# The last stage of a twelve-layer kernel: branch first, eight places, two queues, one root for all tiles

## The chip, the cores and the metric

The kernel runs on one core of one Trainium2 chip. The core has five engines with a queue of instructions each: TensorE (PE, with its weight loads PEld), VectorE (DVE), ScalarE (ACT), GpSimd (POOL) and SyncE (SP), which here only issues transfers. Transfers are issued from the queues of SP, ACT and POOL and carried out by the core's 16 DMA engines. The metric is the time of one execution in microseconds of the device; the median of several executions counts. Profiles come from one more execution each.

## The reference, cut to what matters

The program is a stack of four levels, each with a cross attention, an attention and a feed-forward layer with experts, on 1024 rows (32 x 32) of 256 columns. The change is in the last layer alone:

```python
def _rmsnorm(x, w):
    var = jnp.mean(x * x, axis=-1, keepdims=True)
    return w * (x * jax.lax.rsqrt(var + EPS_NORM))
...
src = x + _gqa(x, qw, qb, kw, kb, vw, vb, ow, ob)
src = _rmsnorm(src, norm1_w)
src = src + _moe(src, gate_w, w1, w2)
return _rmsnorm(src, norm2_w)
...
x = x + _L3_ffn_ref(...)
return x
```

`_moe` sends every row to two of eight experts and adds their two results, weighted, to the row.

## The kernel before, in words

The 1024 rows lie in eight tiles of 128 rows by 256 columns: `self.x` holds the running result, `r.h` (called `src` in the last layer; the program's name for its storage is `rows`) the layer's own copy, four tiles in each of two buffers. NT is 8, HT is 4, NH is 2, K is 2.

The last layer, `l3_ffn`, does its attention and norm, and scatters the rows into places by expert. `experts` (from line 1973) runs over eight slots: it loads weights and rows on SP's queue, multiplies on PE, and writes each result row to the table `yk` in HBM, by indirect transfers from POOL's queue (line 2009). What follows is the stretch that the change rewrites:

- `outputs` (lines 2126 to 2134), still within the pool of the experts: for each of the eight tiles, SP loads the two result rows of each row from `yk` (256 KB, tile `gy`, four places in turn, line 2132), and VectorE adds them with their weights to `r.h`, one instruction for each k (line 2134).
- `rest` (lines 2136 to 2154): the general case in which an expert got more rows than its slot holds. A flag is computed early; every engine loads it (line 2151), compares and jumps (line 2152). With these inputs the body is jumped over. An engine that jumps then writes its semaphore up by what the body would have added; others wait for these values.
- `rms_half` (lines 2350 to 2359), once for each half of four tiles: four squares with sums on ACT (line 2356), the root by `rsqrt` on VectorE (lines 152 to 157, eleven small instructions on 128x4), four products with root and row on VectorE, in place (line 2359).
- four additions to `x` on POOL for each half (line 2409).
- in `tile_perceiver`, eight stores from SP (line 2428).

The instructions are recorded through a framework that places semaphores and tracks which buffers are in use; where no order is fixed by hand (`tc.manual_schedule`), it may put independent instructions of one engine in another order, as it does with the two halves' roots. When a pool is closed and another one opened on the same memory, the first writer of the new one waits for all users of the old one. Line 2491 is the end of the program: SP waits for the semaphores of all transfers, every engine drains, and they meet at a barrier.

Of the kernel before, what the change touches and what calls it, by code (L numbers as in the profile page):

```python
# [17 lines left out]
AF = mybir.ActivationFunctionType  # L18
ALU = mybir.AluOpType
# [3 lines left out]
P = 128  # L23
B, S, D = 32, 32, 256
NT = B * S // P
NH = 2
HT = NT // NH
# [40 lines left out]
class Kernel:  # L68
# [78 lines left out]
    def rsqrt(self, var, n, eps, scale=1.0):  # L147


        nc = self.nc  # L150
        a, r, u = (self.t(self.small, [P, HT], x)[:, 0:n] for x in ("rs_a", "rs_r", "rs_u"))
        nc.vector.tensor_scalar(a, var, scale, eps, ALU.mult, ALU.add)  # L152
        nc.vector.tensor_scalar(r.bitcast(I32), a.bitcast(I32), -0.5, float(0x5F3759DF), ALU.mult, ALU.add)  # L153
        for _ in range(3):
            nc.vector.tensor_mul(u, r, r)  # L155
            nc.vector.scalar_tensor_tensor(u, u, -0.5, a, ALU.mult, ALU.mult)  # L156
            nc.vector.scalar_tensor_tensor(r, u, 1.5, r, ALU.add, ALU.mult)  # L157
        return r
# [2199 lines left out]
        for i, s in enumerate(tiles):  # L2358
            nc.vector.scalar_tensor_tensor(s, s, r[:, i : i + 1], row, ALU.mult, ALU.mult)  # L2359

    def l3_ffn(self):
        nc, a, tc = self.nc, self.a, self.tc
        pre = "L3_ffn_"
        vb, ob, n1, n2 = (self.load_row(pre + n) for n in ("vb", "ob", "norm1_w", "norm2_w"))
        gw = self.load_w(a[pre + "gate_w"], "gw", 1)
        net = lambda r: (512, a[pre + "w1"], a[pre + "w2"], None, AF.Gelu, r.h, None)
        with tc.tile_pool(name="f3r", bufs=1) as outer:
            r = self.routing(outer, 8, 2, ((3, 112),) * 4 + ((2, 112), (2, 80), (1, 128), (1, 64)), CAPACITY)
            src = r.h
            hT = self.norm_T(self.x, src)  # L2370
            hT2 = []
            for i in range(NT):
                nc.gpsimd.tensor_tensor(src[i], src[i], ob, ALU.add)

            def end(i, ps):
                nc.vector.tensor_tensor(src[i], ps, src[i], ALU.add)

            def done(t0, n):

                part = slice(t0, t0 + n)  # L2380
                self.rms_half(src[part], n1)
                if t0 % HT == 0:
                    hT2.append(self.t(self.act, [P, 2, 512], "hT", 3))
                for i, s in enumerate(src[part]):
                    self.transpose_tile(s, hT2[-1], (t0 + i) % HT * P)
                W = [P, n, 8]
                pr, comb = r.lg[:, part, :], r.comb[:, part, :]
                self.gates(pr, hT2[-1], gw, 8, None, t0 % HT)
                nc.scalar.activation(pr, pr, AF.Sigmoid)
                m, _ = self.top(outer, pr, 8, 2, r.before[:, part, :])  # L2390
                nc.vector.tensor_tensor(comb, pr, m, ALU.mult)
                s = self.t(self.small, [P, HT], "wo_r", 1)[:, 0:n]
                nc.vector.reduce_sum(s, comb, axis=AX.X)
                nc.vector.tensor_scalar(s, s, 1e-6, None, ALU.add)
                nc.vector.reciprocal(s, s)
                nc.vector.tensor_tensor(comb, comb, s.unsqueeze(2).to_broadcast(W), ALU.mult)
                self.route(r, t0, n, m)

            self.qk_attn(pre, ("qw", "kw", "vw", "ow"), hT, pre + "qb", pre + "kb", vb, self.soft_max(0.25), False, end, done)
            with tc.tile_pool(name="f3m", bufs=1) as pool:  # L2400
                self.big = pool
                self.experts(pool, r, *net(r))
                self.outputs(pool, r, r.h, range(NT))
            self.rest(r, hT2, *net(r))
            for hf in range(NH):
                half = src[hf * HT : (hf + 1) * HT]
                self.rms_half(half, n2)
                for s, x in zip(half, self.x[hf * HT : (hf + 1) * HT]):
                    nc.gpsimd.tensor_tensor(x, x, s, ALU.add)  # L2409


@with_exitstack
def tile_perceiver(ctx: ExitStack, tc: tile.TileContext, a: dict, out: bass.AP):
    k = Kernel(ctx, tc, a)
    k.setup()
    k.load_ctx()
    k.xattn_heads(0)
    k.same_rows()
    k.clear_places()
    k.l0_attn()  # L2420
    k.l0_ffn()
    k.l1()
    k.l2()
    k.xattn_one()
    k.l3_attn()
    k.l3_ffn()
    for i in range(NT):
        tc.nc.sync.dma_start(out[i * P : (i + 1) * P, :], k.x[i])


# [64 lines left out]
```

## Time and profile before

| what | value |
|---|---|
| median of three runs | 1991.59 us (1985.03 to 1997.29) |
| the profiled execution's own time | 1987.18 us |
| its span | 1985.4 us |
| instructions | 40586 |
| busy share of the span: PE, DVE, ACT, POOL | 78%, 52%, 29%, 22% |
| granted TensorE clock, mean | 0.872 |
| last scatter to `yk` issued (line 2009) | 1951.25 us from the span's start |
| first load of `gy` issued (line 2132) | 1954.94 |
| last store issued (line 2428) | 1980.0 |

A time within the span is counted from the span's start. A line of the timeline gives start, length, engine, line of the code, operation, what is written and read, how many instructions were merged, and in brackets the idle time before it with what ended it. SPq, ACTq and the like are an engine's queue: transfers, branches and semaphores rather than computation. The page's shares are averages over all layers; this change has to be read from the last 35 us.

### The profile page before, as it was taken

What the parts mean: (1) busy time and instruction counts of PE and PEld (TensorE: products, weight loads), DVE (VectorE), ACT (ScalarE), POOL (GpSimd) and SP (SyncE); (2) the same over time, 40 slices, a digit from 0 to 9 for tenths busy, and PEclk for the clock granted to TensorE, in tenths of its full rate; (3) what the DMA queues carried; (4) which work ended last, traced back from release to release, by engine and by line L of the source; (5) the groups of instructions that cost most, each with busy time, mean ns of one, the idle gap of its engine ahead of it and who ended that gap; (6) DMA issues with size and microseconds to landing.
All of it is one profiled execution on the core that took longest, in us unless ns stands there. A gap on an engine that the chain in (4) does not pass through costs nothing. (4 is left out here: it accounts for less than half of the span.)

```text
span 1985.4 us, 40586 instructions
## 1 busy us (share of the span) xinstructions
PE 1543.9 (78%) x16098; PEld 1073.2 (54%) x16098; DVE 1031.1 (52%) x3295; ACT 582.4 (29%) x1631; POOL 433.0 (22%) x467
## 2 busy tenths in 40 slices
PE   6888879767999698766399689996894758777492
PEld 3555556544678365545277456655563634445372
DVE  6787764554111577656722264548624345555514
ACT  2443435521322366522122133430010212212121
POOL 2222211213011244330412211111312320120322
PEclk9999989876999899887699879998996979876596
DMA  9600001204443321011447621101102632000233
GB/s 279 189 2 1 7 22 44 71 8 146 139 145 112 129 66 55 26 64 60 149 155 212 184 83 41 33 25 52 27 13 74 207 119 86 2 2 2 92 124 116
DMA packets 117879, 167.01 MB, mean 84 GB/s; under 512 B 20272, under 2 KB 79676, under 8 KB 117664
## 3 DMA queue, kind: packets, MB, share of 16 engines
q1 hardware_dynamic: 106352, 140.59, 23.0%
q0 software_dynamic: 8144, 17.75, 2.5%
q10 hardware_dynamic: 3168, 5.79, 0.8%
q8 instruction: 137, 2.24, 0.5%
q14 instruction: 78, 0.64, 0.1%
HBM read 118.55 MB, written 48.84 MB: 84 GB/s over the span
## 5 line engine op out<-in xcount | busy, mean ns | idle before, releaser
L106 PE MATMUL mm<-e,hid 128*128 128x256 f32 (+4 forms) x984 | 231.2, 384 | 0.2
L106 PEld LDWEIGHTS mm<-e,hid 128*128 128x128 f32 (+4 forms) x984 | 172.4, 179 | 39.1 <-issue 1.3
L106 PE MATMUL sc<-xT,e 128*128 128x256 f32 (+8 forms) x736 | 179.8, 394 | 17.4 <-issue 12.8
L2009 POOL DMA_INDIRECT yk<-ys,to x98 | 92.8, 947 | 360.4 <-DVE ys L2007 189.4
L106 PEld LDWEIGHTS sc<-xT,e 128*128 128x128 f32 x736 | 130.0, 194 | 61.0 <-issue 24.7
L576 POOL TENSOR_TENSOR p<-p,over 128x512 f32<-128x512 f32 x80 | 102.8, 1293 | 254.6 <-DVE over L574 237.0
L563 ACT ACTIVATE p<-sc,less 128x256 f32<-128x256 f32 x256 | 117.9, 476 | 80.5 <-DVE less L555 49.0
L1879 POOL DMA_INDIRECT xg<-rows,pl_at x72 | 71.3, 990 | 223.7 <-DVE pl_at L1875 134.5
L106 PE MATMUL mm<-hT,w 128*128 128x512 f32 (+1 forms) x272 | 110.6, 566 | 7.7 <-ACT hT L356 7.7
L2110 ACT ACTIVATE hid<-sc,b1s 128x256 f32<-128x256 f32 (+6 forms) x152 | 72.2, 475 | 127.6 <-PE sc L106 126.6
L106 PE MATMUL mm<-ctxA,w 128*128 128x256 f32 x256 | 78.9, 427 | 18.8 <-DVE aT L607 7.4
L2007 DVE TENSOR_TENSOR ys<-mm,b2r 128x512 f32<-128x512 f32 (+6 forms) x44 | 28.2, 641 | 124.7 <-PE mm L106 124.3
L552 DVE TENSOR_REDUCE most<-sc 128x4 f32<-128x1024 f32 x64 | 77.9, 1217 | 18.6 <-PE sc L106 18.6
L106 PEld LDWEIGHTS mm<-hT,w 128*128 128x128 f32 x272 | 58.4, 221 | 52.2 <-issue 38.4
L584 PE MATMUL mm<-ident,p 128*128 128x128 f32 x512 | 77.7, 291 | 11.3 <-DVE aT L607 9.5
L2091 DVE TENSOR_TENSOR mine<-xs,or_one 112x24 f32<-112x24 f32 (+13 forms) x32 | 5.9, 184 | 147.5 <-DMA xs<-xg 147.5
L106 PE MATMUL mm<-w,ctxA 128*128 128x256 f32 x256 | 73.8, 409 | 6.5 <-DVE pT L585 3.6
L584 PEld LDWEIGHTS mm<-ident,p 128*128 128x128 f32 x512 | 57.9, 147 | 33.7 <-issue 12.1
L2087 PE MATMUL mm<-ident,xs 128*128 128x128 f32 (+3 forms) x196 | 30.2, 286 | 54.0 <-DMA xs<-xg 35.2
L585 DVE COPY pT<-mm 128x512 f32<-128x512 f32 x96 | 63.3, 685 | 15.4 <-PE mm L584 15.2
L106 PE MATMUL mm<-w,hT 128*128 128x256 f32 x224 | 70.9, 457 | 0.0
L106 PE MATMUL mm<-w,soT 128*128 128x256 f32 x128 | 51.2, 539 | 24.7 <-DVE soT L1576 18.1
(453 smaller groups left out, 3028.0 us busy)
## 6 DMA issues: line engine op xcount, KB each, us to landing
e<-in_L_ffn_w SPq DMA_DIRECT2D x16, 1024.0 KB, 6.9
e<-in_L_ffn_W SPq DMA_DIRECT2D x32, 512.0 KB, 4.8
rows<-kR SPq DMA_DIRECT2D x32, 384.0 KB, 3.3
xg<-zero SPq DMA_DIRECT2D x8, 1088.0 KB, 12.7
kt<-kT SPq DMA_DIRECT2D x32, 256.0 KB, 3.2
e<-in_L_ffn_w SPq DMA_DIRECT2D x16, 512.0 KB, 4.4
gy<-yk SPq DMA_DIRECT2D x24, 256.0 KB, 3.3
kR<-rows SPq DMA_DIRECT2D x16, 384.0 KB, 2.5
```

The costliest lines, as they stand in the source:

```text
L106: self.nc.tensor.matmul(out, lhsT, rhs, start=start, stop=stop)
L552: nc.vector.reduce_max(mx, sc.rearrange("p r (o k) -> p r o k", o=2), axis=AX.X)
L563: nc.scalar.activation(p[:, g, o, :], sc[:, g, o * 256 : o * 256 + 256], AF.Exp, bias=less[:, g, o : o + 1], scale=scale, accum_out=sums[: ...
L576: eng.tensor_tensor(p[:, g], p[:, g], r[:, g].unsqueeze(2).to_broadcast([P, 2, 256]), ALU.mult)
L584: nc.tensor.transpose(tp[:, r * P : (r + 1) * P], ps_[r // 2][:, r % 2, o, j * P : (j + 1) * P], self.ident)
L585: copies[j](pT[:, j].rearrange("p r t -> p (r t)"), tp)
L1879: ins = nc.gpsimd.indirect_dma_start(out=r.places, out_offset=bass.IndirectOffsetOnAxis(ap=at[:, t, k : k + 1], axis=0), in_=mine[:, t, :] ...
L2007: nc.vector.tensor_tensor(dst, src, b2r[0:n, :].unsqueeze(1).to_broadcast([n, len(js), D]), ALU.add)
L2009: ins = nc.gpsimd.indirect_dma_start(out=self.yk[0:choices, :], out_offset=bass.IndirectOffsetOnAxis(ap=to[0:n, j : j + 1], axis=0), in_=y ...
L2087: nc.tensor.transpose(tp[:, c * P : c * P + n], xs[0:n, j, c * P : (c + 1) * P], self.ident[0:n, 0:n])
L2091: nc.vector.tensor_tensor(mine[0:n, 0:nj, :], xs[0:n, 0:nj, D : D + E], r.one[0:n, s, :].unsqueeze(1).to_broadcast([n, nj, E]), ALU.mult)
L2110: nc.scalar.activation(hid[:, mm, 0:rows], ps[:, mm % 2, 0:rows], func, **kw)
```

## The change: what it does

- `rest`, the branch, now stands ahead of the loads and sums. They are no longer in the experts' pool but in a pool of their own that is opened after the branch.
- All eight `gy` tiles have a place of their own, and the loads alternate between the queues of SP and ACT.
- VectorE and ACT follow a written order: sums of all eight tiles on VectorE, each tile's square on ACT behind them.
- POOL multiplies each finished tile of `r.h` with the norm's row into a new tile (`by_row`), eight instructions.
- One root on 128x8 takes the place of two on 128x4. For that, the buffers in `rsqrt` are eight columns wide everywhere.
- One VectorE instruction a tile then does product with the root and addition to `x`; POOL's eight additions are gone.
- The stores alternate between SP and ACT too, four each.

Behind the branch, the first loads on both queues, the first sum and the first product wait for the semaphores of all hardware transfers and of the other engines' branches, besides the last scatter. The order of every other instruction on every engine is the same.

```diff
@@ rsqrt
-        a, r, u = (self.t(self.small, [P, HT], x)[:, 0:n] for x in ("rs_a", "rs_r", "rs_u"))
+        a, r, u = (self.t(self.small, [P, NT], x)[:, 0:n] for x in ("rs_a", "rs_r", "rs_u"))
@@ l3_ffn
                 self.experts(pool, r, *net(r))
-                self.outputs(pool, r, r.h, range(NT))
             self.rest(r, hT2, *net(r))
-            for hf in range(NH):
-                half = src[hf * HT : (hf + 1) * HT]
-                self.rms_half(half, n2)
-                for s, x in zip(half, self.x[hf * HT : (hf + 1) * HT]):
-                    nc.gpsimd.tensor_tensor(x, x, s, ALU.add)
+            self.last_outputs(r, n2, out)
+
+    def last_outputs(self, r, row, out):
+        nc, tc, K = self.nc, self.tc, r.K
+        eng = mybir.EngineType
+        queue = (nc.sync, nc.scalar)
+        with tc.tile_pool(name="f3y", bufs=1) as pool:
+            gs = [self.t(pool, [P, K * D], f"gy{t}") for t in range(NT)]
+            sqs = [self.t(pool, [P, D], f"sq{i}") for i in range(2)]
+            ws = [self.t(pool, [P, D], f"by_row{t}") for t in range(NT)]
+            ss = self.t(pool, [P, NT], "squares")
+            for t, g in enumerate(gs):
+                queue[t % 2].dma_start(g, self.yk[t * K * P : (t + 1) * K * P, :].rearrange("(p k) d -> p (k d)", k=K))
+            with tc.manual_schedule(engines={eng.DVE, eng.Activation}):
+                for t, g in enumerate(gs):
+                    for k in range(K):
+                        nc.vector.scalar_tensor_tensor(r.h[t], g[:, k * D : (k + 1) * D], r.by[:, t, k : k + 1], r.h[t], ALU.mult, ALU.add)
+                    nc.scalar.activation(sqs[t % 2], r.h[t], AF.Square, accum_out=ss[:, t : t + 1])
+                    nc.gpsimd.tensor_tensor(ws[t], r.h[t], row, ALU.mult)
+                roots = self.rsqrt(ss, NT, 1e-6, 1.0 / D)
+                for t, x in enumerate(self.x):
+                    nc.vector.scalar_tensor_tensor(x, ws[t], roots[:, t : t + 1], x, ALU.mult, ALU.add)
+            for t, x in enumerate(self.x):
+                queue[t % 2].dma_start(out[t * P : (t + 1) * P, :], x)
@@ tile_perceiver
-    k.l3_ffn()
-    for i in range(NT):
-        tc.nc.sync.dma_start(out[i * P : (i + 1) * P, :], k.x[i])
+    k.l3_ffn(out)
```

More of the change, by code (lines that the diff above doesn't have):

```diff
@@ L2359, in rms_half, with l3_ffn @@
             nc.vector.scalar_tensor_tensor(s, s, r[:, i : i + 1], row, ALU.mult, ALU.mult)
-    def l3_ffn(self):
+    def l3_ffn(self, out):
         nc, a, tc = self.nc, self.a, self.tc
```

## The prediction, made before the run

> **What bounds the kernel now.** The edit touches only what follows the last expert, so I read the chain of waits first (which work ended last), then the timeline of the last 40 us, then the branch, the closing lines and the DMA by stage. The chain runs through the very instructions that the edit rewrites:
>
> ```profile
> 1970.87 2.56 DVE rows L2359 x4
> ...
> 1976.68 2.63 POOL x L2409 x3
> 1979.31 0.68 POOLq L2491
> ```
>
> The timeline has the whole stretch (start, length, engine, line):
>
> ```profile
> 1951.25 0.92 POOL L2009 DMA_INDIRECT yk<-ys,to  x1 [0.76 <-ACT ys L114]
> 1954.94 7.17 SPq L2132 DMA_DIRECT2D gy<-yk  x8
> 1957.71 1.92 DVE L2134 SCALAR_TENSOR_TENSOR rows<-gy,by,rows 128x256 f32<-128x256 f32 x4 [8.48 <-DMA gy<-yk]
> ...
> 1964.50 1.92 DVE L2134 SCALAR_TENSOR_TENSOR rows<-gy,by,rows 128x256 f32<-128x256 f32 x4 [0.49 <-SPq L2152]
> 1966.91 0.42 ACT L2356 ACTIVATE h<-rows 128x256 f32<-128x256 f32 x1 [15.94 <-DVEq L2152]
> ...
> 1968.64 0.17 DVE L152 TENSOR_SCALAR rs_a<-rms_s 128x4 f32<-128x4 f32 x1 [2.23 <-ACT h L2356]
> ...
> 1970.82 2.61 DVE L2359 SCALAR_TENSOR_TENSOR rows<-rows,rs_r,row 128x256 f32<-128x256 f32 x4
> ...
> 1972.31 8.04 SPq L2428 DMA_DIRECT2D out<-x  x8
> ...
> 1976.68 3.31 POOL L2409 TENSOR_TENSOR x<-x,rows 128x256 f32<-128x256 f32 x4 [1.99 <-DVE rows L2359]
> ```
>
> So the path is: last scatter issued 1951.25, landed when SP issues the first load at 1954.94; load; accumulation 1957.71 to 1966.42; branch; squares from 1966.91; root from 1968.64; norms and additions 1970.82 to 1979.99; last output issued at 1980.0. All of it is 30.5 us of a span of 1985.4. Two things more have to be seen. VectorE and GpSimd hold each other up (narrow windows of the timeline), and GpSimd's closing drain (the groups of line 2491) lasts long:
>
> ```profile
> 1970.82 0.48 DVE L2359 SCALAR_TENSOR_TENSOR rows<-rows,rs_r,row 128x256 f32<-128x256 f32 x1
> 1971.39 0.89 POOL L2409 TENSOR_TENSOR x<-x,rows 128x256 f32<-128x256 f32 x1 [19.22 <-DVE rows L2359]
> 1971.62 0.95 DVE L2359 SCALAR_TENSOR_TENSOR rows<-rows,rs_r,row 128x256 f32<-128x256 f32 x1
> 1972.24 0.90 POOL L2409 TENSOR_TENSOR x<-x,rows 128x256 f32<-128x256 f32 x1
> 1973.35 0.68 DVE L155 TENSOR_TENSOR rs_u<-rs_r 128x4 f32<-128x4 f32 x1
> ```
>
> ```profile
> L2491 POOLq DRAIN  x3: 45/113/5808, 1978.8 to 1985.1; - x3
> L2491 SPq DRAIN  x3: 7/7/13, 1982.1 to 1984.8; - x3
> ```
>
> A norm of 0.48 us takes 0.95 beside GpSimd: it ends 1972.57, 0.28 after the addition ended (1972.28); the next addition ends 0.57 after that (1973.14); and an operation on 4 columns takes 0.68 instead of 0.16. So the two take turns: GpSimd's turn is some 0.58, VectorE's 0.28, and the rest of each instruction (0.14 and 0.20) overlaps. The drain runs 1978.8 to 1984.6, 4.6 us past GpSimd's last addition and 2.5 past SP, which had its outputs' semaphores at 1982.1; then 0.8 to the end.
>
> **The change, part by part.**
>
> **Branch ahead of the outputs.** Today ACT's first square waits for VectorE's branch: 1966.42 to 1966.91, 0.49 us on the path. Moved, the branch runs on each engine after its last expert instruction. Rows of line 2152: PE's comparison 1948.6 lasts 3469 ns and its semaphore is written at 1952.2; ACT's 1951.0 and 1951.4; VectorE is free at 1949.2 and took 0.9 from flag load to semaphore; SP is free from 1944.6. The first loads now wait for all of these and for the last scatter (landed 1954.94), which ends last by 2.7 us. The longest gaps from comparison to semaphore at the two earlier branches are 2.6 on ACT (631.0 to 633.6) and 2.9 on VectorE (1127.2 to 1130.1); even those would end by 1953.6. So -0.45 (0.04 remains as ACT's wake-up). Added: some ten semaphore waits in pairs ahead of the first load and first sum; those that stand behind the scatter's cost 0.06 each (SP's at its closing line), so +0.15; bounds 0 and 0.4.
>
> **Eight places, two queues.** Today SP issues four loads, then waits for VectorE to free a place. That late supply costs VectorE three waits, 0.21 + 0.33 + 0.49 = 1.03. They go: the loads' own pace is full DMA, 256 KB in 0.64 to 0.75:
>
> ```profile
> 1957.00:1958.00 1.00, 0.00 (x0) 0.00 (x0) 0.29 (x1) 0.00 (x0) 0.00 (x0) 0.50 1.01 359
> 1958.00:1959.00 1.00, 0.00 (x0) 0.00 (x0) 0.96 (x3) 0.00 (x0) 0.00 (x0) 0.50 0.99 320
> ```
>
> (the last two columns are DMA share and GB/s), against 0.92 of VectorE's work a tile. But the first two tiles now start together on two queues and share the engines. Today the first landed 2.75 after issue and the second 3.0, at 1958.33. If both end together, the first sum starts at 1958.33 plus the 0.15 above, 1958.5: +0.8 (bounds 0, if the first tile goes through alone, and 1.2). The Trainium skill, "DMA: Bandwidth & Descriptors", Queues, rings and completion order, has each DMA engine go round the queues packet by packet. By that the two first tiles do land together, the +0.8; by one queue's order the sum would be 0.65 less. No row here shows two queues loading at once with nothing else.
>
> **Products by GpSimd during the sums.** 16 sums of 0.48 in pairs of 0.92 are 7.4 us alone. Eight products (GpSimd, two SBUF inputs, 128x256, as line 2409: 0.72 alone) each start 0.09 after a tile's second sum. By the turns above, the next tile's first sum has its turn (ends 0.40 after), the product takes 0.58 (to 0.98), and the second sum waits and ends 0.28 later: 1.26 a tile instead of 0.92. So 1.0 + 7 x 1.26 = 9.8 (bounds 7.4, and 0.92 + 7 x (0.92 + 0.72) = 12.4 if each product excluded VectorE for its whole length). I take 9.8, the turns as the rows show them. The sums end at 1958.5 + 9.8 = 1968.3, 1.9 later than 1966.42.
>
> The bound has a page to it. The Trainium skill, "SBUF — State Buffer", SBUF: two separate sides, says that a GpSimd operation and a VectorE operation with two SBUF inputs exclude each other for the whole instruction. By that the sums end 2.6 later still. The rows agree with the exclusion, but put it at 0.58 of the 0.72.
>
> **Squares and one root.** Seven of eight squares lie under the sums; ACT has nothing else to do. After the last sum: one square with its sum, 0.51, wake-ups 0.08, and about 0.1 because the last product (until 0.8 after the last sum) holds the root's first instruction: root at 1969.0. The root takes 2.18 as now (1968.64 to 1970.82; 8 columns cost what 4 do, since 16 to 24 columns also take 0.17). Gone: three exposed squares (1.2) and the second root, during which everything stood after 1974.7.
>
> **One last instruction a tile.** Eight, free of each other, spaced 0.40 as line 2359's unhindered ones, GpSimd silent by then: 7 x 0.40 + 0.48 = 3.3 (3.8 if each keeps 0.48). They end 1971.2 + 3.3 = 1974.5, and the last output is issued there, 5.5 ahead of 1980.0. Outputs now leave at 0.40 spacing, 128 KB each, 330 GB/s, about what the DMA rows carry at most: 0.3 on the landing of 1.7.
>
> **The close.** GpSimd's last instruction is now a product ending at 1969.1; its drain, if it follows that by 4.6 as today, is over at 1973.7 and waits for nothing. So after the last output: 1.7 + 0.3 landing, 0.45 of SP's semaphores, 0.8 barrier: 1977.75.
>
> **Sum:** 1985.4 - 1977.75 = 7.65 us less span: 5.5 from the tail's work, 2.1 from the drain. The profiled execution took 1987.18 (span plus 1.78), so 1979.5 for it. It is 4.4 under the median of the three runs, 1991.59 (1985.03 to 1997.29). A new median will fall within that spread; I set the gain against the mean of all four executions, 1990.3: **1982.6**.
>
> **Rivals** (all at that level).
> 1. *Products exclude VectorE for their whole length.* For: 0.68 instead of 0.16 on a tiny instruction. Against: the 0.28 and 0.57 above. Gain 7.65 - 2.6 = 5.0: 1985.3.
> 2. *The drain does not follow GpSimd's last work but stands at the end whatever comes.* For: only GpSimd's outlasts its engine; VectorE's 2643 ns from 1976.1 ends with its last norm. Against: nothing else of GpSimd's is open. Gain 5.5: 1984.8.
> 3. *Products fit into VectorE's gaps for nothing.* Against: the narrow windows. The sums take 7.4, gain 10.0: 1980.3.
> 4. *Slower: the branch ahead of the loads is not covered.* Every engine's loads and sums stand behind it, and one jump's late instructions hold all. For: 2.5 to 3.7 between comparison and semaphore in several rows. Against: 2.7 us of cover here. It decides when a branch ends later than 1962.6, 11.6 after ACT's comparison, three times the longest row; one of 14 us gives +2.3: 1992.6.
>
> **How the numbers follow.** Forecast 0.50, rival 1 0.20, rival 2 0.15, rival 3 0.12, rival 4 0.03. The mechanisms span 1980 to 1985; the executions before spread 6 us either way around their mean, and a median of a few narrows that little. So 1974 to 1990 for 8 in 10. A measurement of this kernel can tell about 1% from no change, 20 us; the whole stretch after the last scatter has 30.5, of which I find 8, and rival 4 would need far more than any row. So faster by over 1% 0.03, within 1% 0.95, slower 0.02.
>
> **What would show it.** Loads on SP and ACT issued near 1955, not later: branch covered. Sums: pairs of about 1.26 with second sums near 0.8, products 0.7 to 0.9: turns. VectorE's waits for loads gone after the first. One root, eight last instructions at 0.40. GpSimd's drain ended before the last output has landed: the 2.1. I am wrong if the first load starts after 1956, if the sums take over 11 us, or if the end follows the last output by 5 us as now.

## The result, and the profile after

| | before | after |
|---|---|---|
| median, 14 runs each | 1990.24 us (1981.86 to 1997.29) | 1982.93 us (1973.06 to 1995.27) |
| profiled execution, its span | 1987.18, 1985.4 | 1978.80, 1976.9 |
| last scatter issued, to the end of the span | 34.16 | 26.50 |

The ratio is 0.9967, with a 95% interval of 0.9951 to 0.9982: some 7 us of 1990, which is real and within the 1% that counts as no change. The prediction was 1982.6.

The timeline of the changed kernel shows the same stretch as the one shown of before (start, length, engine, line):

```profile
1950.44 0.92 POOL L2009 DMA_INDIRECT yk<-ys,to  x1 [0.76 <-ACT ys L114]
1952.72 2.37 ACTq L2417 DMA_DIRECT2D gy<-yk  x4
1952.76 2.35 SPq L2417 DMA_DIRECT2D gy<-yk  x4
1956.73 2.27 DVE L2421 SCALAR_TENSOR_TENSOR rows<-gy,by,rows 128x256 f32<-128x256 f32 x4 [8.30 <-DMA gy<-yk]
...
1959.44 7.46 DVE L2421 SCALAR_TENSOR_TENSOR rows<-gy,by,rows 128x256 f32<-128x256 f32 x12 [0.45 <-DMA gy<-yk]
1960.68 0.90 POOL L2423 TENSOR_TENSOR by_row<-rows,row 128x256 f32<-128x256 f32 x1 [0.88 <-DVE rows L2421]
...
1961.94 0.90 POOL L2423 TENSOR_TENSOR by_row<-rows,row 128x256 f32<-128x256 f32 x1 [0.36 <-DVE rows L2421]
...
1966.98 0.72 POOL L2423 TENSOR_TENSOR by_row<-rows,row 128x256 f32<-128x256 f32 x1 [0.36 <-DVE rows L2421]
...
1967.54 0.20 DVE L152 TENSOR_SCALAR rs_a<-squares 128x8 f32<-128x8 f32 x1 [0.63 <-ACT sq L2422]
...
1969.86 3.26 DVE L2426 SCALAR_TENSOR_TENSOR x<-by_row,rs_r,x 128x256 f32<-128x256 f32 x8
1970.37 2.71 SPq L2428 DMA_DIRECT2D out<-x  x4
1970.77 2.71 ACTq L2428 DMA_DIRECT2D out<-x  x4
```

Read it by the predicted steps. Both queues issue within 2.3 us of the last scatter, 1.0 after the branch's last row (TensorE's semaphore at 1951.7): the branch is covered. From the third tile on there is no wait for a load between sums. The third to seventh product start 1.26 apart (1960.68, 1961.94) and last 0.90; the last one, with nothing beside it, takes 0.72, as does the second, half of which lies in VectorE's wait for the third tile. One root, eight last instructions in 3.26 us. The groups of the closing line show GpSimd's drain, which was the end of the kernel before (1978.8 plus 5808 ns, after SP's first row of 1982.1), now well ahead of SP's:

```profile
L2508 POOLq DRAIN  x3: 45/113/5352, 1966.9 to 1976.7; - x3
L2508 SPq DRAIN  x3: 7/7/13, 1976.1 to 1976.4; - x3
```

It ends at 1966.9 + 5.35 = 1972.3, 3.8 us before SP has seen its outputs land (1976.1). The chain of waits agrees: behind the scatter GpSimd is no longer in it (two of its lines):

```profile
1953.16 6.26 DMA gy<-yk
...
1970.74 2.38 DVE x L2426 x6
```

One table carries all that follows. Each column is a stage of the tail, read from the timelines; the first four add up to the fifth, and the fourth is called the close below. "Drain" is the time from GpSimd's last work to the end of its drain. The scatter's landing (issue to first load) is kept apart: it was 2.3 us in four of these profiled executions (after, a3, c1, d3) and 3.7 to 4.4 in the other nine, kernels of both kinds among them.

| kernel | first load to first sum | sums | last sum to last VectorE | from there to the end | first load to end | drain |
|---|---|---|---|---|---|---|
| before | 2.77 | 8.71 | 12.31 | 6.68 | 30.47 | 4.59 |
| after | 4.01 | 10.17 | 6.20 | 3.83 | 24.22 | 4.59 |
| a1: a late copy on GpSimd | 4.02 | 9.83 | 6.20 | 5.67 | 25.73 | 4.59 |
| a2: no products | 4.11 | 7.42 | 6.11 | 3.79 | 21.43 | 5.20 |
| a3: sums in PSUM | 4.13 | 7.92 | 6.20 | 3.93 | 22.18 | 4.59 |
| a4: loads on one queue | 3.14 | 9.84 | 6.21 | 3.49 | 22.68 | 4.59 |
| b1: before, branch ahead | 3.21 | 8.51 | 8.84 | 6.68 | 27.23 | 4.59 |
| b2: before, additions on VectorE | 2.78 | 7.99 | 12.11 | 3.45 | 26.34 | 5.36 |
| b3: four places | 4.02 | 9.83 | 6.22 | 3.85 | 23.91 | 4.59 |
| c1: a3 and a4 together | 3.21 | 8.71 | 6.20 | 3.68 | 21.81 | 4.59 |
| d1: b1 and b2 together | 3.35 | 7.74 | 8.63 | 3.44 | 23.17 | 5.62 |
| d2: branch behind the sums | 3.87 | 7.42 | 10.91 | 3.04 | 25.24 | 4.59 |
| d3: two roots | 4.15 | 9.85 | 8.23 | 3.71 | 25.94 | 4.59 |

By the table the change saves 30.47 - 24.22 = 6.25 us. The 7.66 that the two profiled executions differ by from the last scatter on (34.16 against 26.50) hold another 1.41 of the scatter's landing (3.69 against 2.27). Their spans differ by 0.8 more, which lies ahead of the last scatter, where the edit changes only the width of the root's buffers.

What separates the two landings can be seen in the packets of the transfers. In the nine late ones, a transfer of 16 KB on queue q8, which the profile calls an instruction transfer, is under way, and what is left of the scatter (queue q0) starts within 0.02 us of its end. In the four others that transfer starts only after the scatter's last packet has ended. The DMA view of the kernel before in two windows, from 1952.80 to 1952.90 and from 1953.86 to 1954.20 (queue, kind: packets that start there, MB, share of the 16 engines):

```profile
q8 instruction: 1, 0.02, 66.2%
```

```profile
q0 software_dynamic: 2, 0.00, 4.7%
```

The first starts at 1952.84 and ends at 1953.90; the scatter's two start at 1953.89 and 1954.11. In the changed kernel the scatter's last packet ends at 1952.21 and that transfer starts at 1952.78. No edit aims at it, and what sets its start stays open, so the 1.41 us are luck for the prediction.

### The profile page after: what moved, and what is told of

Its sections match the earlier page's. It is cut to its first block, busy times and chain, and to the rows that moved or that the text cites. A ratio compares the mean times of both kernels' runs of the same rounds, so it can differ in the third digit from the quotient of the medians.

```text
span 1976.9 us, 40595 instructions
## 1 busy us (share of the span) xinstructions
PE 1543.9 (78%) x16098; PEld 1075.4 (54%) x16098; DVE 1029.1 (52%) x3284; ACT 583.3 (30%) x1631; POOL 433.1 (22%) x467
## 3 DMA queue, kind: packets, MB, share of 16 engines
q10 hardware_dynamic: 4320, 7.37, 1.1%
## 5 line engine op out<-in xcount | busy, mean ns | idle before, releaser
L106 PE MATMUL sc<-xT,e 128*128 128x256 f32 (+8 forms) x736 | 183.9, 400 | 14.8 <-issue 13.7
L106 PEld LDWEIGHTS mm<-ctxA,w 128*128 128x128 f32 x256 | 46.9, 204 | 42.0 <-issue 18.7
```

The costliest lines, as they stand in the source:

```text
L106: self.nc.tensor.matmul(out, lhsT, rhs, start=start, stop=stop)
```

## The experiments

Effects of one to three microseconds can't be told apart by whole times that spread by more than that from one execution to the next, so single times are not compared; the stages of the table are. Sets ran on different chips, and the kernel before took 1995 us beside the a kernels and 2013 in median beside the others; so of the kernels below only c1 and d1, which were timed repeatedly, are given a ratio.

### a1: does the drain follow GpSimd's last work?

```diff
             for t, x in enumerate(self.x):
                 nc.vector.scalar_tensor_tensor(x, ws[t], roots[:, t : t + 1], x, ALU.mult, ALU.add)
+            last = self.t(pool, [P, 1], "last_copy")
+            nc.gpsimd.tensor_copy(last, self.x[NT - 1][:, 0:1])
```

The copy is added work that leads nowhere.

> The changed kernel with one more GpSimd instruction, a copy of one column that waits for the last VectorE instruction. It leads nowhere. Theory (GpSimd's closing drain follows its own last work by 4.6 us): the drain ends 4.6 to 4.8 us after that copy, and the span ends about 5.7 us after the last VectorE instruction instead of 3.8, so 1.9 us later. Rival (the drain is long for another cause, or counts from something else): the end stays 3.8 us after the last VectorE instruction.

Timeline and groups of the closing line of a1:

```profile
1982.70 0.19 POOL L2428 COPY last_copy<-x 128x1 f32<-128x1 f32 x1 [5.47 <-DVE x L2426]
```

```profile
L2510 POOLq DRAIN  x3: 45/113/4798, 1982.7 to 1988.0; - x3
L2510 SPq DRAIN  x3: 7/7/13, 1985.7 to 1987.7; - x3
```

0.19 us of GpSimd's work at the end move the end by 1.84 (5.67 against 3.83): the drain ends 4.59 after the copy, at 1987.5, 1.8 after SP's first row. Rival 2 of the prediction, a drain that stands at the end whatever comes, is out.

### a2 and a3: what the products cost the sums, and by what

a2 leaves out the product with the norm's row (the last instruction reads `r.h` in place of `by_row`); its time is that of a smaller computation.

```diff
-                    nc.gpsimd.tensor_tensor(ws[t], r.h[t], row, ALU.mult)
...
-                    nc.vector.scalar_tensor_tensor(x, ws[t], roots[:, t : t + 1], x, ALU.mult, ALU.add)
+                    nc.vector.scalar_tensor_tensor(x, r.h[t], roots[:, t : t + 1], x, ALU.mult, ALU.add)
```

> The changed kernel without GpSimd's eight products: it leaves out the multiplication with the norm's row, the last instruction of a tile reads the layer's own row instead. Theory (GpSimd and VectorE take turns, 0.34 us a product): the sums take 16 x 0.46 = 7.4 us plus a wait for loads of up to 0.8, so 7.5 to 8.2 instead of 10.2; the span from the first sum to the end is 2 to 2.5 us shorter, as GpSimd's drain starts earlier still. Rival (the sums are spaced by the loads' arrival, the products cost nothing): the sums still take about 10 us, with waits for loads in them.

a3 keeps the products, but gives every sum one input in PSUM: TensorE, idle here, copies the rows there first.

```diff
+            banks = [self.mm_ps() for _ in range(NT // 2)]
+            hs = [banks[t // 2][:, t % 2 * D : t % 2 * D + D] for t in range(NT)]
+            for t in range(NT):
+                self.mm(hs[t], self.ident, r.h[t])
...
-                    for k in range(K):
-                        nc.vector.scalar_tensor_tensor(r.h[t], g[:, k * D : (k + 1) * D], r.by[:, t, k : k + 1], r.h[t], ALU.mult, ALU.add)
+                    for k, (a, b) in enumerate(((hs[t], hs[t]), (r.h[t], hs[t]))):
+                        nc.vector.scalar_tensor_tensor(a, g[:, k * D : (k + 1) * D], r.by[:, t, k : k + 1], b, ALU.mult, ALU.add)
```

> The changed kernel with the layer's rows copied into PSUM by TensorE (eight products with the unit matrix, 128x256, while the loads are under way) and the sums reading them there, so that each sum has one input in SBUF instead of two. The products on GpSimd stay. Theory (it is the two SBUF inputs that exclude GpSimd): pairs take 0.92 to 1.0 us although GpSimd runs beside them, products 0.72, sums in all about 7.6 to 8.4 instead of 10.2 us; some 2 us less to the end. Rival (any VectorE work beside GpSimd's product is held up, or the sums wait for something else): pairs stay at 1.26 us.

The sums in a2, all sixteen in one line of the timeline:

```profile
1962.44 7.42 DVE L2420 SCALAR_TENSOR_TENSOR rows<-gy,by,rows 128x256 f32<-128x256 f32 x16 [10.10 <-DMA gy<-yk]
```

Two tiles of a3, with the products of the tiles before beside them:

```profile
1961.73 0.49 DVE L2425 SCALAR_TENSOR_TENSOR mm<-gy,by,mm 128x256 f32<-128x256 f32 x1
1961.78 0.72 POOL L2427 TENSOR_TENSOR by_row<-rows,row 128x256 f32<-128x256 f32 x1 [0.19 <-DVE rows L2425]
1962.26 0.48 DVE L2425 SCALAR_TENSOR_TENSOR rows<-gy,by,mm 128x256 f32<-128x256 f32 x1
1962.66 0.48 DVE L2425 SCALAR_TENSOR_TENSOR mm<-gy,by,mm 128x256 f32<-128x256 f32 x1
```

Without products a tile takes 0.92 and all 7.42: the work alone, with no wait for a load. In the changed kernel a tile takes 1.26 and a product 0.90. In a3 both run, and neither is held up: the product takes its own 0.72, a sum 0.48, a tile 0.98 on average (1961.73 to 1962.66 is 0.93, the next 1.03). So the 0.34 a tile that the products cost are neither GpSimd's time nor a transfer, but what the two engines' SBUF inputs do to each other; with one of VectorE's two inputs in PSUM it is gone, also for each tile's second sum, which still writes to SBUF. The Trainium skill, "SBUF — State Buffer", SBUF: two separate sides, names that condition, two SBUF inputs against a GpSimd operation that reads SBUF, and a3 agrees with it. The page's "whole instruction" does not hold here: by it a tile would take 0.92 + 0.72 = 1.64, and 1.26 were measured. Rival 1 of the prediction (12.4 us of sums) is out, and so is rival 3 (products for nothing): 10.17 lies 2.75 above a2's 7.42, of which 0.45 is a wait for the third tile's load that a1 and a4 did not have.

### a4: one queue for the loads

```diff
-                queue[t % 2].dma_start(g, self.yk[t * K * P : (t + 1) * K * P, :].rearrange("(p k) d -> p (k d)", k=K))
+                nc.sync.dma_start(g, self.yk[t * K * P : (t + 1) * K * P, :].rearrange("(p k) d -> p (k d)", k=K))
```

> The changed kernel with all eight loads on SP's queue; stores still alternate. Theory (two queues share the same DMA engines, so the second queue only makes the first two tiles land together): the first sum starts 0.4 to 0.7 us sooner after the first load's issue (about 3.4 us instead of 4.0), the sums end at the same time or up to 0.6 sooner, as VectorE's own 1.26 a tile bounds them. Rival (one queue cannot issue fast enough, and two gave a gain): VectorE waits for loads between tiles, and the sums end 0.5 us or more later.

Timeline of a4:

```profile
1960.23 3.67 SPq L2417 DMA_DIRECT2D gy<-yk  x8
1963.38 9.84 DVE L2421 SCALAR_TENSOR_TENSOR rows<-gy,by,rows 128x256 f32<-128x256 f32 x16 [9.15 <-DMA gy<-yk]
```

The first 3.2 us from the first load by windows, of a4 and of a1, which has two queues (the last two columns are the share of the DMA engines' time and GB/s):

```profile
1960.20:1963.40 3.20, 0.00 (x0) 0.00 (x0) 0.03 (x1) 0.00 (x0) 0.00 (x0) 0.50 0.60 185
```

```profile
1962.60:1965.80 3.20, 0.00 (x0) 0.00 (x0) 0.00 (x0) 0.00 (x0) 0.00 (x0) 0.50 0.58 217
```

The first sum begins 3.14 after the first load instead of 4.01, and the sums then take no longer. Where the branch stands ahead, the table has this four times and six times: with one queue 3.14 to 3.35 (a4, b1, c1, d1), with two 4.01 to 4.15. Nor do two queues clearly move more in the same time: 173 to 221 GB/s over the first 3.2 us in seven profiles, against 185 to 210 with one queue (113 in c1, see there). Two tiles come at once, and VectorE can use one. By the Trainium skill, "DMA: Bandwidth & Descriptors", Queues, rings and completion order, the engines go round the queues packet by packet, and the rows agree with what follows from that. In a1 the last packets of the first two tiles end 0.17 us apart, in a4 0.92. So this part of the change costs 0.87 us (4.01 against 3.14), more than the prediction's 0.65.

### b1: the branch ahead, and nothing else

```diff
                 self.experts(pool, r, *net(r))
-                self.outputs(pool, r, r.h, range(NT))
             self.rest(r, hT2, *net(r))
+            with tc.tile_pool(name="f3y", bufs=1) as pool:
+                self.outputs(pool, r, r.h, range(NT))
```

This is an edit of the kernel before.

> The kernel before with the branch of the overflow pass moved ahead of the outputs, and nothing else (four places, one queue, two roots, GpSimd's additions). If the branch is covered by the experts' last work, the gap from the last sum to the first root falls from 2.23 us to about 1.8 (0.45 less: VectorE and ScalarE no longer pass the branch there), and first load to end from 30.5 to 30.0; the first load is issued no more than 0.15 us later after the last scatter's landing. Rival, the branch is not covered: the first load begins some 3.5 us after the last scatter has landed, since TensorE's comparison and branch take that long, and the whole is 3 us longer. Second rival: the gap of 2.23 us is ScalarE's squares alone, and nothing is gained.

Timeline of b1 from the first sum:

```profile
1974.67 4.68 DVE L2134 SCALAR_TENSOR_TENSOR rows<-gy,by,rows 128x256 f32<-128x256 f32 x10 [8.99 <-DMA gy<-yk]
...
1975.71 0.42 ACT L2356 ACTIVATE h<-rows 128x256 f32<-128x256 f32 x1 [8.29 <-DVE rows L2134]
...
1980.10 0.17 DVE L152 TENSOR_SCALAR rs_a<-rms_s 128x4 f32<-128x4 f32 x1
...
1983.81 0.17 DVE L152 TENSOR_SCALAR rs_a<-rms_s 128x4 f32<-128x4 f32 x1
```

From the view of line 2134 (duration in ns, first and last start), VectorE's waits ahead of that first sum:

```profile
L2134 DVEq EVENT_SEMAPHORE  x5: 49/50/50, 1974.2 to 1974.6; - x5
```

None of the three expectations: the gain is 3.24, not 0.45 (27.23 against 30.47), and 3.47 from the last sum to the last VectorE instruction (8.84 against 12.31). In the kernel before ScalarE's first square waited for VectorE's branch, and VectorE came to the branch only behind its last sum; so all eight squares, and both roots behind them, stood after the sums. In b1 ScalarE's first square runs 1.0 us after the first sum began, the first half's root begins while sums are still running (1980.10; the last sum ends 1983.17), and the second half's 0.64 after the last sum instead of 4.09. The branch was a fence between two stages that could overlap, and the 0.49 us at the fence itself were the small part of it. The pool that comes with the edit is not the cause: d2, below, keeps it, and the fence is back.

The branch ahead also has a price, which the expectation leaves out: first load to first sum takes 3.21 instead of 2.77. Five rows of semaphore waits, 0.10 apart, now stand between the first tile's landing and the first sum; the kernel before has none there.

### b2: the eight additions on VectorE, and nothing else

```diff
                 for s, x in zip(half, self.x[hf * HT : (hf + 1) * HT]):
-                    nc.gpsimd.tensor_tensor(x, x, s, ALU.add)
+                    nc.vector.tensor_tensor(x, x, s, ALU.add)
```

Also an edit of the kernel before.

> The kernel before with the last eight additions on VectorE instead of GpSimd. If the end of the kernel before was GpSimd's drain (it ends 4.6 us after GpSimd's last work), the drain is now over long before the last output, and the end follows the last VectorE instruction by 3.5 to 3.9 us as in the changed kernel, not by 6.7; VectorE's own work from the first root to its last instruction stays near 10 us (eight additions of about 0.40 more, but eight products of 0.40 to 0.45 instead of about 0.65 since GpSimd no longer takes turns with them): first load to end about 27.5 to 28, some 2.5 us less than before. Rival, the end is set by the last output's landing and the drain only stands beside it: the end follows the last output's issue by 5.4 us as it did, and the whole gains 0.7 us or nothing.

Its second half's products by the timeline, and GpSimd's drain:

```profile
1993.02 1.67 DVE L2359 SCALAR_TENSOR_TENSOR rows<-rows,rs_r,row 128x256 f32<-128x256 f32 x4
```

```profile
L2491 POOLq DRAIN  x3: 45/113/5887, 1969.5 to 1999.2; - x3
```

The drain now follows the last scatter and is over at 1975.4; the end comes 3.45 after the last VectorE instruction instead of 6.68. VectorE does twice the instructions in about the same time (12.11 against 12.31), because four products take 1.67 here and 2.61 beside GpSimd. That is the first theory. The whole, 26.34, is better than the 27.5 expected, since the sums also ran with fewer waits for loads (7.99 against 8.71), which this edit does not touch.

### d1: b1 and b2 together

The edits of b1 and b2, and no other: four places, one queue, two roots, the old products.

> The kernel before with two of its edits only: the branch ahead of the outputs, and the last eight additions on VectorE, so that GpSimd has nothing to do there; four places, one queue, two roots and the old products stay. If the two effects that were seen alone add up (branch ahead: 27.2 us from the first load to the end instead of 30.5; additions on VectorE: the end 3.45 us after the last VectorE instruction instead of 6.7), first load to end is 23.8 to 24.3 us, as long as the whole change needs (24.2), and the ratio to before is 0.995 to 0.998. Rival, VectorE becomes the bound once it has the additions too (two roots 4.3, eight products 3.3, eight additions 2.9 behind the last sums): the last VectorE instruction then comes 10 us after the last sum instead of 8.8, and first load to end is 25.2 or more.

Timeline of d1, the first root, while sums are still running (the last ends at 1984.96), and the last four additions:

```profile
1982.21 0.17 DVE L152 TENSOR_SCALAR rs_a<-rms_s 128x4 f32<-128x4 f32 x1
...
1992.17 1.43 DVE L2410 TENSOR_TENSOR x<-x,rows 128x256 f32<-128x256 f32 x4
```

The two add up: 3.24 + 4.13 = 7.37 expected from the stages, 30.47 - 23.17 = 7.30 found. That is below the range on record, whose lower end of 23.8 counted the drain's 3.2 alone of b2's gain: the other 0.7 were shorter waits for loads, and they came again here (sums 7.74, with 8.71 before), though neither edit aims at them. The ratio is 0.9948 (0.9928 to 0.9969); its interval overlaps that of the whole change, so the times alone don't rank them, but the stages do: the rest of the change adds 1.05 us to d1. It comes from four terms: sums 10.17 against 7.74 (+2.43), last sum to last VectorE instruction 6.20 against 8.63 (-2.43), first sum +0.66, close +0.39. Products on GpSimd with one root and one last instruction take about as much in the sums (0.45 of it a wait for a load) as they save behind them; what is lost is the first sum's delay, which goes with the second queue (a4), and the close, whose cause is open.

### d2: the changed kernel with the branch put back behind the sums

```diff
-            self.rest(r, hT2, *net(r))
-            self.last_outputs(r, n2, out)
+            self.last_outputs(r, n2, out, lambda: self.rest(r, hT2, *net(r)))
...
-            with tc.manual_schedule(engines={eng.DVE, eng.Activation}):
+            with tc.manual_schedule(engines={eng.DVE}):
                 for t, g in enumerate(gs):
...
+            rest()
+            with tc.manual_schedule(engines={eng.DVE, eng.Activation}):
+                for t in range(NT):
                     nc.scalar.activation(sqs[t % 2], r.h[t], AF.Square, accum_out=ss[:, t : t + 1])
                     nc.gpsimd.tensor_tensor(ws[t], r.h[t], row, ALU.mult)
```

> The changed kernel with the branch put back between the sums and the squares. If the branch is a fence (in the kernel before no square begins until VectorE has passed it, 0.5 us after the last sum), the sums run without products beside them (7.4 to 7.9 us instead of 10.2), but then eight squares of 0.40 stand between the last sum and the root, which begins 4.0 us after the last sum instead of 0.63; the products run beside the squares and the root; the last VectorE instruction comes 9.6 to 9.9 us after the last sum, and first load to end is 25.0 to 25.4 us, 1 us more than the changed kernel. Rival, by the prediction's step that costs the branch at 0.45 us: squares and products still run beside the sums, and first load to end is 24.7 with sums of 10.2.

Timeline of d2:

```profile
1987.77 7.42 DVE L2420 SCALAR_TENSOR_TENSOR rows<-gy,by,rows 128x256 f32<-128x256 f32 x16 [9.72 <-DMA gy<-yk]
1995.70 0.42 ACT L2424 ACTIVATE sq<-rows 128x256 f32<-128x256 f32 x1 [15.92 <-DVEq L2152]
1995.81 5.50 POOL L2425 TENSOR_TENSOR by_row<-rows,row 128x256 f32<-128x256 f32 x8 [14.83 <-DVEq L2152]
...
1999.04 0.26 DVE L152 TENSOR_SCALAR rs_a<-squares 128x8 f32<-128x8 f32 x1 [3.84 <-ACT sq L2424]
```

The fence again: squares and products both wait for VectorE's branch (the releaser in the brackets), the root begins 3.84 after the last sum, and the products slow the root down in turn (3.8 us from its first instruction to the first last instruction, 2002.85, instead of 2.32). 25.24 lies in the first theory's range, but by two misses that cancel: 10.91 from the last sum to the last VectorE instruction where 9.6 to 9.9 were expected, and a close of 3.04 where the changed kernel has 3.83. Here the move of the branch is worth only 1.02 (25.24 against 24.22): it saves 4.71 behind the sums, and 2.75 of that go to the products that it lets under the sums, 0.79 to the close and 0.14 to the first sum. So the price of moving it depends on what is behind it: 3.24 where squares and a root follow, 1.02 where the product of another engine follows as well.

The short close is worth a look, because d2 stores just as the changed kernel does, on two queues, 0.40 apart. The stores' rate in 40 slices, of the changed kernel (1970 to 1975.4) and of d2 (2003 to 2008.1), and the one transfer that only the first has there:

```profile
GB/s 0 0 0 0 0 0 0 0 8 296 341 281 281 357 342 311 341 296 342 326 372 319 341 311 387 303 289 342 311 289 334 364 213 30 23 23 15 23 23 0
q14 instruction: 1, 0.01, 0.9%
```

```profile
GB/s 0 0 0 0 0 0 0 0 0 137 361 329 249 321 329 338 314 361 305 314 345 345 322 345 337 314 337 337 346 337 337 290 345 361 169 0 0 0 0 0
```

In the changed kernel some 0.8 us of packets at a low rate follow the bulk, in d2 none. The last store's packets end 2.15 after its issue there, 1.38 here.

### b3: four places, and d3: two roots

b3 is the changed kernel with `gy{t % 4}` for `gy{t}`; d3 has the root in halves:

```diff
-                roots = self.rsqrt(ss, NT, 1e-6, 1.0 / D)
-                for t, x in enumerate(self.x):
-                    nc.vector.scalar_tensor_tensor(x, ws[t], roots[:, t : t + 1], x, ALU.mult, ALU.add)
+                for hf in range(NH):
+                    roots = self.rsqrt(ss[:, hf * HT : (hf + 1) * HT], HT, 1e-6, 1.0 / D)
+                    for t in range(HT):
+                        x = self.x[hf * HT + t]
+                        nc.vector.scalar_tensor_tensor(x, ws[hf * HT + t], roots[:, t : t + 1], x, ALU.mult, ALU.add)
```

> The changed kernel with four places for the loads instead of eight, so that the fifth to eighth load wait for the sums of the first to fourth tile. The kernel before, with four places, lost 1.3 us in VectorE's waits for loads (sums 8.7 us long where 7.4 are work). Here a pair of sums takes 1.26 us with GpSimd's turns, longer than the loads' pace in the kernel before (about 1.1 us a tile), so these waits should be mostly hidden: sums 10.2 to 10.7 us long against 10.2. Rival, eight places are worth their full 1.3 us: sums of 11.5 us, and VectorE waits for gy at every tile from the fifth on.

> The changed kernel with a root for each half, both behind the last sum: root, four last instructions, root, four last instructions. If the chain of eleven small instructions is what a root costs, whatever its width, the last VectorE instruction comes 2.0 to 2.3 us later after the first root began (7.6 to 7.9 us instead of 5.6), and since the first four outputs are issued earlier the close is 3.5 to 3.8 us: first load to end 26.0 to 26.5 us instead of 24.2. Rival, the close is set by eight outputs landing together, and the earlier first half gives back a part: close 3.0 us or less, first load to end 25.5 or less.

Timelines of b3 and of d3:

```profile
1979.10 7.85 SPq L2417 DMA_DIRECT2D gy<-yk  x4
1983.08 9.83 DVE L2421 SCALAR_TENSOR_TENSOR rows<-gy,by,rows 128x256 f32<-128x256 f32 x16 [10.26 <-DMA gy<-yk]
```

```profile
1988.80 1.67 DVE L2428 SCALAR_TENSOR_TENSOR x<-by_row,rs_r,x 128x256 f32<-128x256 f32 x4
...
1990.39 0.17 DVE L152 TENSOR_SCALAR rs_a<-squares 128x4 f32<-128x4 f32 x1
...
1992.65 1.67 DVE L2428 SCALAR_TENSOR_TENSOR x<-by_row,rs_r,x 128x256 f32<-128x256 f32 x4
```

b3: the later loads do wait for their place (SP's four issues are spread over 7.85 us), and VectorE's sixteen sums still run without a wait between them, 9.83 long, under the 10.2 to 10.7 expected. With a tile every 1.26 us, four places are enough; the eight are worth nothing here (what the waits for them were worth in the kernel before, the products' turns now hide). d3: 8.23 from the last sum to the last VectorE instruction instead of 6.20. One root is worth 2.0 in this order of work, and nothing of it comes back at the close (3.71).

### c1: a3 and a4 together

One line from each: sums in PSUM, loads on SP's queue alone.

> The changed kernel with the sums of the last layer gathered in PSUM (TensorE copies the rows there first) and all eight loads on SP's queue. If both effects seen one at a time add up: first sum about 3.1 us after the first load is issued, sums 7.9 us long, 6.2 us from the last sum to the last VectorE instruction, 3.5 to 3.8 us from there to the end: 20.7 to 21.0 us from the first load to the end, where the changed kernel took 24.2 and the kernel before 30.5. That is about 3.3 us less than the changed kernel and 9.6 less than before, less 1.2 us if the last scatter lands as late after its issue as before: 1980 to 1981 us, a ratio of about 0.995. Rival: with shorter sums the single queue's loads become the bound (eight issues of 0.43 us, the last landing some 3 us behind its issue): then the sums take about 8.5 to 9 us and VectorE shows waits for gy, and 1 us of the 3.3 is lost.

Timeline of c1:

```profile
1978.98 4.22 SPq L2417 DMA_DIRECT2D gy<-yk  x8
1982.19 0.49 DVE L2425 SCALAR_TENSOR_TENSOR mm<-gy,by,mm 128x256 f32<-128x256 f32 x1 [7.55 <-DMA gy<-yk]
...
1984.02 0.49 DVE L2425 SCALAR_TENSOR_TENSOR mm<-gy,by,mm 128x256 f32<-128x256 f32 x1 [0.82 <-DMA gy<-yk]
```

The ratio is 0.9949 (0.9929 to 0.9969), and first load to end 21.81, the shortest of the kernels that do the whole computation, 2.4 less than the changed kernel and 0.8 to 1.1 more than expected. The sums take 8.71, as in the rival, with a wait of 0.82 for the second tile; from first load to last sum c1 takes 11.92 and a3 12.05, so in this profile hardly anything is left of the single queue's gain. The rival's reason, a queue that can't keep up, is not shown by it. In a4, on the same single queue, the second tile's sums start 0.92 after the first's, without a wait. In c1 the transfers themselves slowed down. From 2.5 to 3.5 us after the first load, c1 and then a4:

```profile
1981.50:1982.50 1.00, 1.00 (x5) 0.79 (x4) 0.31 (x1) 0.00 (x0) 0.00 (x0) 0.58 0.49 82
```

```profile
1962.70:1963.70 1.00, 0.00 (x0) 0.00 (x0) 0.33 (x1) 0.00 (x0) 0.00 (x0) 0.50 0.90 266
```

What slowed them one profile does not tell, so whether one queue is fast enough for sums from PSUM stays open.

## Why the prediction was right, step by step

The time came out as forecast, 1982.6 and 1982.93, and so did the mechanisms but for the branch's. That the sum agrees to the hundredth, 7.65 forecast and 7.66 in the profiled pair from the last scatter on, is luck: the tail from the first load saved 6.25 instead of the 7.8 that the forecast's terms give (30.47 less 22.65, which is 3.4 + 9.8 + 6.2 + 3.25 for the four columns), and the scatter happened to land 1.41 sooner. The medians differ by 7.3, with an interval of about 3.6 to 9.8 by the ratio, and so can't tell 6.25 from 7.65. The miss of 1.6 has three places: 0.6 in the first sum, 0.4 in the sums, 0.6 in the close.

- **Branch, -0.45.** Covered, as said, by 1.0 us where 2.7 were forecast, mostly since the scatter landed early. But this was the step with the wrong reading. It took one wait of 0.49 for the branch's price and booked the squares that run under the sums, and the earlier root, to a step of their own. b1 moves the branch alone and has 3.24 of the gain, with no written order. The sum didn't suffer, since every square was counted once. An answer to "which part of this change is worth having" would have been wrong by it.
- **Loads.** First sum after first load: 3.4 forecast, 4.01 measured. The mechanism, two tiles that share the engines, is borne out by a4 and the table; it was sized at 0.65 and is 0.87. The other part is the semaphore waits behind the branch, a term of 0.15 with an upper bound of 0.4: in b1 those ahead of the first sum alone cost 0.44. The waits of 1.03 did go, but b3 shows that four places do without them as well.
- **Products.** 1.0 + 7 x 1.26 = 9.8 was forecast. Where no load was late (a1, a4, b3) the sums take 9.83 and 9.84; in the changed kernel's profile another 0.45 is a wait for the third tile. The turns that two rows of another stage showed carry over to this one to the hundredth.
- **Squares and root, last instructions.** 0.63 from the last sum to the root (0.7 forecast), 2.32 for the root (2.18: its eleven instructions are a little longer on eight columns, 0.17 to 0.20 instead of 0.16), 3.26 for eight last instructions (3.3). d3 prices the one root at 2.0.
- **The close.** The drain is off the path (a1). From the last VectorE instruction to the end it takes 3.83, where 3.25 was forecast from the last output's issue: SP's first drain comes 2.9 after that issue (1973.15 to 1976.06) instead of 2.45, and the rest takes 0.9 instead of 0.8. Beside the loads this is the largest part of the miss, and nearly all of it is the last output's landing: its packets end 2.15 after its issue (1.35 in the kernel before). Two queues are not the reason by themselves, as d2 lands in 1.38 with the same stores. What goes with it is a transfer of 8 KB on queue q14 (1973.37 to 1974.13 in the changed kernel), again called an instruction transfer: the eight profiles in which one starts between 1.3 us before the last store's issue and 0.7 after it have landings of 1.85 to 2.19, the five others 1.35 to 1.43. No run tried it by itself.
- **Rivals.** 1 is out by a3 and by 1.26 a tile, 2 by a1 and b2, 3 by a2, 4 by the loads' times.

Of the 6.25, then: the branch and the additions alone give 7.30 (d1), of which 1.0 are shorter waits for loads that neither edit aims at, and everything else in the change takes 1.05 back: the products and the one root with its one last instruction about even out, the second queue loses, the eight places do nothing. Two things stay open: whether it is the 8 KB transfer that makes the close longer, and what decides when the 16 KB one starts, and with it whether the scatter lands early. Both rest on thirteen single profiles.

## What to carry to other kernels

A branch in the middle of a stage is priced by what it keeps apart, not by the wait at its rows: look up which engine reaches it last and what the others could have done meanwhile. Before an edit moves work to an idle engine, see what that engine shares with the one on the path, and what it must still do at the end: here eight additions on GpSimd cost 3.2 us at the close and slowed VectorE, and products on it cost the sums about as much as they saved later. By the stages of single profiles the whole change gained 6.25 us and two small edits of it 7.30, so run the parts.

## What the runs showed of the hardware that was not expected

- GpSimd's drain ended 4.59 us after the engine's last computation in all ten kernels where that was a product, an addition or a 0.19 us copy, and 5.20 to 5.62 after the last scatter's instruction where that was the last work (a2, b2, d1).
- TensorE's comparison at the branch took 3.4 to 4.0 us in every kernel (row of line 2152: 3616 to 3863 ns in the changed kernel), other engines' 45 to 72 ns. It is hidden here by the last scatter.
- A VectorE instruction with one input in PSUM and one in SBUF ran beside GpSimd at its full 0.48 to 0.49 us, and GpSimd beside it at 0.72 to 0.73; with both inputs in SBUF, a tile's second sum took 0.83 and the product 0.90.
- A second queue delayed the first sum by 0.87 us (after against a4), with no clearly higher transfer rate over the first 3.2 us (198 and 185 GB/s).
- What was left of the last scatter started within 0.02 us of the end of a 16 KB instruction transfer in nine profiles, and the first load came 3.7 to 4.4 us after the scatter's issue; in the four where that transfer started later it came after 2.3.
